# Mamba block with gated experts on one core: the second block's first stages earlier in the written-out order, and the last output stored by chunk

## The chip, the core and the metric

The kernel runs on 1 core of a Trainium2 chip. The core has five engines with a queue of instructions each, worked off in order: TensorE (PE, matrix products and transposes; its weight loads are listed as PEld), VectorE (DVE), ScalarE (ACT, functions from tables that are loaded by an instruction of its own), GpSimd (POOL), and SyncE (SP), which here issues nearly all DMA transfers. Engines wait for one another through semaphores.

The metric is the device time of one execution in microseconds. Before the change it is 2382.32 us, the median of 4 runs (2381.58 to 2382.68).

## What is computed

The input x is 8 sequences of 2048 tokens with 256 channels, all float32. Per sequence, six vectors of modulation (`sa, ca, ga, sb, cb, gb`) come from a condition vector. A Mamba layer (state space model with convolution) and a layer of 8 gated experts follow, each behind a layer norm with modulation, each added to x through a gate:

```python
h = _layernorm(x, axis=-1) * (1 + ca) + sa
x = x + ga * _L0_attn_ref(h, ...)
h = _layernorm(x, axis=-1) * (1 + cb) + sb
x = x + gb * _L0_ffn_ref(h, ...)

# _L0_attn_ref
zxbcdt = hidden_states @ W_in
z, xBC, dt = ...
xBC = jax.nn.silu(_causal_dwconv(xBC, conv_w, conv_b))
dt = jax.nn.softplus(dt + dt_bias)
A = -jnp.exp(A_log)
y = _ssd(x, dt, A, Bm, Cm) + x * D[None, None, :, None]
y = y * jax.nn.silu(z)
y = y * jax.lax.rsqrt(jnp.mean(y * y, axis=-1, keepdims=True) + EPS) * norm_w
return y @ W_out

# _L0_ffn_ref
gate_logits = jax.nn.softmax(x @ gate_w + gate_b, axis=-1)
weights = gate_logits * (gate_logits >= THRESHOLD)
weights = weights / sum(weights)
for e in range(E):
    out = out + weights[:, e:e + 1] * (x @ expert_w[e] + expert_b[e])
```

`_ssd` is the scan over chunks of tokens: within a chunk a masked product of C and B with decays, between chunks a state that is carried on.

## The kernel before

A block is 512 tokens of one sequence (`T`), four chunks of 128 tokens each (`NC`); there are 32 blocks (`order`), four to a sequence. Each block goes through stages, written as generators: `fetch` (the load of x), `first_norm`, `project_xbc` (the six parts of x, B and C, each followed by `conv`, and `steps_of_time` for dt), `project_z`, `silu_xbc`, for each chunk `spread` (the cumulated decays, written to DRAM as `cs_d` and read back to all partitions as `wide`) and `within` (the chunk's products and the state), after each second chunk `outputs`, then `output` (the projection back, added to x), `gate_weights` and `experts`.

No engine chooses what to do. The order is made when the program is built: each stage is put on a list with a due time (`at`), `yield` puts it back by so many units, and `run` always continues the stage that is due first (lines 190 to 204). Blocks start 70 units apart (`PERIOD`, line 802), and each stage has its offset in `STARTS` (line 803). The units are a plan, not microseconds; what they set is the order of the instructions, which the framework may still shift by a few places when it places them on the queues. On the chip an instruction runs when those ahead of it on its engine have been issued and what it waits for is there.

The 8 PSUM banks are handed out by `take` and `give` (lines 211 to 227) in the same plan, with a most for each use (`MOST`).

Lines that the prediction's steps touch:

- Line 107, `load`: a block's x, 512 KB in one transfer. `first_x` comes in four transfers (line 143); `second_x` is loaded on line 160, behind the columns of `w_in` for z (line 149), the head vectors (152) and `d_ch` (156). The queue of SP is shared with all other weights (161 to 175), `cs_d` (505), `wide` (523) and the outputs (761).
- Lines 330, 331, `statistics`, on DVE; 325 and 326, `inv_sqrt`, on POOL; 339, `shift`, on DVE; 343, `xn`, on ACT, four times; 353, transposes on PE; 355, `ht` with the modulation, on ACT, twice. `ht` of the first norm (tag `ht0`) has one buffer, that of the second (`ht1`) two, line 349.
- Line 424: the projection to x, B and C on PE, six times two products of 128x512; 474: dt. Line 379: its first tap with ACT, 383: the last three columns kept as `halo`, 387: three more taps on DVE.
- Line 460: the projection to z, four times two products; 447: its silu on ACT.
- Lines 486 to 515: softplus, cumulated sum (502) and turning of the steps of time, with an exp (490), a log (494) and an exp (507) on ACT.
- Line 442: silu of x, B and C, three times on ACT.
- In `within`: 538 (ACT, one piece of `w` for each of 8 heads), 548, 549, 551 (transposes and C times B on PE), 552 and 553 (exp on ACT), 556 `xdt`, 560 `both`, 572 `w` (DVE), 568 `xdec`, 575 `cw`, 589 `state` (POOL), 586 (PE), 598 and 600 `state` (DVE).
- In `outputs`: 618 (PE), 630 and 634 (DVE), 641 (ACT), 643 and 644 (POOL). In `output`: 659, 672 (PE), 681 (DVE).
- In `gate_weights`: 699, 707, 738 (PE), 734 `wt` (DVE). In `experts`: 778, 791 (PE), 748 (DVE), 756 and 758 (POOL), and the store, line 761, once per block when its last chunk is done.

Functions of different table sets that follow one another on ACT (silu, exp, log) have a load of tables between them, `ACT_TABLE_LOAD`, 1.28 us each in the profile.

Of the kernel before, what the change touches and what calls it, by code (L numbers as in the profile page):

```python
# [15 lines left out]
P = 128  # L16
# [9 lines left out]
def kernel(  # L26
# [26 lines left out]
    nc = tc.nc  # L53
# [6 lines left out]
    KD = DM // P  # L60
# [3 lines left out]
    T = 512  # L64
    NC = T // P
# [7 lines left out]
    def new(pool, shape, tag, bufs=None):  # L73
        n_names[0] += 1
        kw = {} if bufs is None else {"bufs": bufs}
        return pool.tile(shape, F32, tag=tag, name=f"{tag}_{n_names[0]}", **kw)
# [19 lines left out]
    blk = ctx.enter_context(tc.tile_pool(name="block", bufs=2))  # L96
# [4 lines left out]
    order = [(b, s) for b in range(B) for s in range(NSB)]  # L101
# [3 lines left out]
    def load(b, s):  # L105
        xt = new(io, [P, NC, DM], "xt")
        nc.sync.dma_start(out=xt, in_=x[b, ts(s, T), :].rearrange("(c p) d -> p c d", p=P))
        return xt

    def columns(dst, src, first, count):  # L110
        nc.sync.dma_start(
            out=dst, in_=src[:, first : first + count].rearrange("(k p) n -> p k n", p=P)
        )
# [32 lines left out]
    with nc.allow_non_contiguous_dma(reason="small vectors, an element or a few per partition"):  # L146
        nc.sync.dma_start(out=conv_w_sb, in_=conv_w.rearrange("(m p) k -> p m k", p=P))
        nc.sync.dma_start(out=conv_b_sb, in_=conv_b.rearrange("(m p) -> p m", p=P))
        columns(w_in_sb[:, :, :DI], w_in, 0, DI)
        for name, v in (("dt_bias", dt_bias), ("a_log", a_log)):  # L150
            for c in range(NC):
                nc.sync.dma_start(
                    out=heads[name][c * QD : c * QD + NH, :], in_=v.unsqueeze(1)
                )
        for q in range(2):
            nc.sync.dma_start(
                out=d_ch[ts(q, HEADDIM), :],
                in_=d_skip.rearrange("(m q) -> q m", q=2)[q].partition_broadcast(HEADDIM),
            )
        second_x = load(*order[1])  # L160
        nc.sync.dma_start(out=norm_sb, in_=norm_w.rearrange("(m p) -> p m", p=P))
        nc.sync.dma_start(out=wo_n, in_=w_out.rearrange("(m p) o -> p m o", p=P))
        for g, part in enumerate((2, 5)):
            columns(wgate[:, :, g, :], wmod, part * DM, DM)
        columns(wpp[1], wmod, 3 * DM, 2 * DM)
        nc.sync.dma_start(
            out=gate_w_sb[:, :, :NE], in_=gate_w.rearrange("(k p) e -> p k e", p=P)
        )
# [23 lines left out]
    def at(time, stage):  # L192
        heapq.heappush(events, (time, n_events[0], stage))
        n_events[0] += 1
# [16 lines left out]
    def take(use, count=1):  # L211
        while True:
            now = clock[0]
            idle = sorted((t, i) for i, t in enumerate(free_at) if t <= now)
            held = sum(h == use and t > now for h, t in zip(holder, free_at))
            if len(idle) >= count and held + count <= MOST[use]:
                break
            yield 0.2
        got = []
        for _, i in idle[:count]:  # L220
            free_at[i], holder[i] = 1e9, use
            got.append(new(psum, [P, 512], f"bank{i}"))
            bank_of[got[-1].tensor.name] = i
        return got[0] if count == 1 else got

    def give(ps):
        free_at[bank_of.pop(ps.tensor.name)] = clock[0] + READ_TIME
# [26 lines left out]
    def condition():  # L254
        for k in range(KD):
            ps = yield from take("m")
            nc.tensor.transpose(ps[:, :B], cond_sb[:, ts(k, P)], ident[:B, :B])
            nc.scalar.copy(ct[:, k, :], ps[:, :B])
            give(ps)
        yield from modulation(0, 30.0)  # L260

    def warm():


        ps = yield from take("m")
        yield 40.9
        for _ in range(WARM):
            nc.tensor.matmul(ps[:, :P], ones, upper, start=True, stop=True)
        give(ps)

    def modulation(half, later=1.0):
        ps = yield from take("m")
        for n in range(2):
            for d in range(KD):
                for k in range(KD):
                    nc.tensor.matmul(
                        ps[:, ts(n * KD + d, B)], wpp[half][:, k, n * DM + d * P :][:, :P],
                        ct[:, k, :], start=(k == 0), stop=(k == KD - 1),
                    )
        yield later  # L280
        for n in range(2):
            nc.vector.tensor_scalar(
                mod_pp[:, 2 * half + n], ps[:, ts(n, KD * B)].rearrange("p (d b) -> p d b", b=B),
                float(n), None, ALU.add,
            )
        give(ps)
# [35 lines left out]
    def inv_sqrt(res, src, scale):  # L322

        n = res.shape[1]
        nc.gpsimd.tensor_scalar(res, src, scale, EPS, ALU.mult, ALU.add)
        nc.gpsimd.tensor_tensor(res, res, neg_half[:, :n], ALU.pow)
# [6 lines left out]
    def modulated(src, mv, b, half, keep):  # L333

        rstd = new(sml, [P, NC], "rstd")
        inv_sqrt(rstd, mv[:, :, 1], 1.0)
        yield 3.0
        shift = new(sml, [P, NC], "shift")
        nc.vector.scalar_tensor_tensor(shift, mv[:, :, 0], -1.0, rstd, ALU.mult, ALU.mult)  # L339
        yield 1.5  # L340
        xn = new(blk, [P, NC, DM], "xn", bufs=1)
        for c in range(NC):
            nc.scalar.activation(  # L343
                xn[:, c, :], src[:, c, :], AF.Identity,
                bias=shift[:, c : c + 1], scale=rstd[:, c : c + 1],
            )
            yield 0.6
        yield 6.0
        ht = new(blk, [P, KD, T], f"ht{half}", bufs=1 + half)
        for d in range(KD):  # L350
            ps = yield from take("m")
            for c in range(NC):
                nc.tensor.transpose(ps[:, ts(c, P)], xn[:, c, ts(d, P)], ident)  # L353
            yield 1.0
            nc.scalar.activation(  # L355
                ht[:, d, :], ps, AF.Identity,
                bias=mod_pp[:, 2 * half, d, b : b + 1],
                scale=mod_pp[:, 2 * half + 1, d, b : b + 1],
            )
            give(ps)  # L360
            yield 0.8
        yield 1.0
        keep["ht", half] = ht
# [155 lines left out]
    def spread(n, c):  # L519

        yield from until(info[n], "cs_d")
        wide = info[n]["wide", c] = new(chk, [P, NH, P], "wide")
        nc.sync.dma_start(
            out=wide, in_=info[n]["cs_d"][c * QD : c * QD + NH, :].partition_broadcast(P)
        )
        yield
# [162 lines left out]
    def gate_weights(n):  # L689
        b, s = order[n]  # L690
        d = info[n]
        yield from until(d, *(("x1", c) for c in range(NC)))
        yield from modulated(d["x"], d["mv"], b, 1, d)
        ht = d["ht", 1]
        yield 4.0
# [48 lines left out]
    def weighted(n, c, e, ps, res):  # L744
        wt = info[n]["wt"]
        per = 512 // DM
        for q in range(per):
            nc.vector.scalar_tensor_tensor(  # L748
                res, ps[:, ts(q, DM)], wt[:, c, e + q : e + q + 1], res, ALU.mult, ALU.add
            )  # L750
            if q == per - 1:
                give(ps)
            yield 0.5
        if e + per == NE:
            b, s = order[n]
            nc.gpsimd.tensor_mul(res, res, gated[b][1][:, 0, :])  # L756
            x1 = info[n]["x"]
            nc.gpsimd.tensor_add(x1[:, c, :], x1[:, c, :], res)
            if c == NC - 1:
                yield 1.5  # L760
                nc.sync.dma_start(
                    out=out[b, ts(s, T), :].rearrange("(c p) d -> p c d", p=P), in_=x1
                )

    def experts(n):
# [38 lines left out]
        (fetch, -20.0), (first_norm, -9.0), (project_xbc, 11.5), (project_z, 42.0),  # L804
        (silu_xbc, 47.5), (output, 128.0), (gate_weights, 156.0), (experts, 198.0),
    )
    at(-30.0, condition())
    at(-30.0, warm())
    at(12.0, head_weights())
# [3 lines left out]
    for n in range(len(order)):  # L813
        start = n * PERIOD
        for stage, delay in STARTS:
            at(start + delay, stage(n))
        if order[n][1] == 0:
            at(start + 40.0, batch_gates(order[n][0]))
        for c in range(NC):
            at(start + c * PERIOD / NC + 44.0, spread(n, c))  # L820
            at(start + c * PERIOD / NC + 54.0, within(n, c))
# [34 lines left out]
```

## Time and profile before

| what | value |
|---|---|
| median of 4 runs | 2382.32 us |
| the profiled execution | 2381.58 us |
| its span, first to last instruction | 2379.8 us |
| PE busy | 2316.2 us, 97% |
| VectorE, ScalarE, GpSimd busy | 76%, 68%, 47% |
| PE busy in the first 20 us | 13.40 us |
| granted PE clock, mean of the span | 0.993 |
| costliest group, experts' products L791 | 962.4 us in 2048 instructions |
| DMA, mean rate | 46 GB/s |

A line of a timeline has the start in us from the start of the span, the duration, the engine, the line of the kernel, the operation, the tiles and shapes, how many instructions are drawn together, and in brackets how long the engine was idle before and what ended the wait. A matmul in float32 is two instructions. The busy time of an engine is an average over stages with different limits; what a change in one stage is worth is read from that stage. Durations in a merged line overlap a little, since instructions are pipelined.

### The profile page before, as it was taken

To read this page: it belongs to the slowest core of one execution; us is meant where nothing else is said; L and a number is where in the kernel's file an instruction comes from. 1 tells how busy PE (TensorE), PEld (TensorE's weight loads), DVE (VectorE), ACT (ScalarE), POOL (GpSimd) and SP (SyncE) were. 2 spreads that over 40 slices of the span, in tenths; PEclk is the share of its full clock that TensorE was granted. 3 is DMA by queue.
4 is the path that set the end of the run, shared out by engine and by line. 5 is a ranking of instruction groups with operands and counts; after the bars stand their busy time and mean duration, and the time that the engine had idled before them with its cause. 6 is when DMAs were issued, how large, how long until landed. Compare 5 with 4: busy or idle time off the path is not lost.

```text
span 2379.8 us, 33341 instructions
## 1 busy us (share of the span) xinstructions
PE 2316.2 (97%) x11632; PEld 1313.1 (55%) x11632; DVE 1816.9 (76%) x4188; ACT 1621.1 (68%) x2950; POOL 1128.1 (47%) x1245
## 2 busy tenths in 40 slices
PE   7889999999999999999999999999999999999998
PEld 4555555555555555555555555555555555555564
DVE  5777877778777787877787777778777787777775
ACT  6878766677666686666776667766776767667720
POOL 3554445453454454454544554544545444545442
PEclk8999999999999999999999999999999999999999
DMA  5111111110111111111110111111111101111100
GB/s 166 46 37 46 38 46 46 45 55 28 46 55 46 45 46 37 46 54 47 45 46 28 55 55 36 55 37 37 55 45 46 46 29 54 46 45 46 38 19 18
DMA packets 64649, 110.50 MB, mean 46 GB/s; under 512 B 7097, under 2 KB 47073, under 8 KB 64481
## 3 DMA queue, kind: packets, MB, share of 16 engines
q1 hardware_dynamic: 64464, 108.35, 13.8%
q8 instruction: 93, 1.52, 0.3%
q14 instruction: 76, 0.61, 0.1%
q10 hardware_dynamic: 16, 0.01, 0.0%
HBM read 89.47 MB, written 18.87 MB: 46 GB/s over the span
## 4 chain that ended last, share of the span: by engine, by line
PE 61%; ACT 10%; POOL 9%; DVE 6%; issue 1%; POOLq 0%; ACTq 0%; DVEq 0%
PE bank L791 26%; PE bank L672 8%; PE bank L424 7%; PE bank L460 6%; PE bank L618 4%; POOL cw L575 3%; PE bank L586 3%; ACT w L538 3%; DVE xbc L387 2%; PE bank L353 1%; PE bank L548 1%; ACT xbc L442 1%; POOL sq L643 1%; POOL xdec L568 1%; ACT wide L552 1%
## 5 line engine op out<-in xcount | busy, mean ns | idle before, releaser
L791 PE MATMUL bank<-we_sb,ht 128*128 128x512 f32 x2048 | 962.4, 595 | 3.3 <-DVE both L560 1.9
L748 DVE SCALAR_TENSOR_TENSOR res<-bank,wt,res 128x256 f32<-128x256 f32 x1024 | 487.5, 476 | 199.8 <-PE bank L791 113.3
L791 PEld LDWEIGHTS bank<-we_sb,ht 128*128 128x128 f32 x2048 | 373.9, 190 | 379.4 <-issue 352.2
L387 DVE SCALAR_TENSOR_TENSOR xbc<-bank,conv_w_sb,xbc 128x511 f32<-128x511 f32 (+2 forms) x576 | 425.8, 740 | 121.1 <-ACT halo L383 119.6
L575 POOL TENSOR_TENSOR cw<-wide,xbc 128x1024 f32<-128x1024 f32 x128 | 310.8, 2428 | 295.5 <-ACT wide L552 168.9
L538 ACT ACTIVATE w<-wide,tok_major 128x128 f32<-128x128 f32 x1024 | 327.9, 390 | 141.8 <-PE bank L618 100.8
L424 PE MATMUL bank<-ht,w_in_sb 128*128 128x512 f32 x768 | 369.5, 604 | 0.9 <-DVE xbc L387 0.8
L460 PE MATMUL bank<-ht,w_in_sb 128*128 128x512 f32 x512 | 244.4, 601 | 0.0
L672 PE MATMUL bank<-wo,zs 128*128 128x256 f32 x1024 | 243.6, 380 | 0.0
L589 POOL TENSOR_TENSOR state<-state,wide 128x512 f32<-128x512 f32 x112 | 121.7, 1086 | 232.9 <-DVE state L600 206.6
L424 PEld LDWEIGHTS bank<-ht,w_in_sb 128*128 128x128 f32 x768 | 140.7, 192 | 154.9 <-issue 139.8
L355 ACT ACTIVATE ht<-bank,mod_pp 128x512 f32<-128x512 f32 x128 | 97.4, 775 | 178.9 <-PE bank L353 178.7
L379 ACT ACTIVATE xbc<-bank,conv_b_sb,conv_w_sb 128x512 f32<-128x512 f32 x192 | 147.2, 766 | 102.7 <-PE bank L424 102.6
L672 PEld LDWEIGHTS bank<-wo,zs 128*128 128x128 f32 x1024 | 189.8, 191 | 49.0 <-issue 23.5
L568 POOL TENSOR_TENSOR xdec<-xdt,tok_major 128x512 f32<-128x512 f32 x120 | 139.8, 1165 | 141.9 <-DVE xdt L556 141.5
L756 POOL TENSOR_TENSOR res<-res,gates 128x256 f32<-128x256 f32 x128 | 134.8, 1053 | 151.8 <-DVE res L748 144.4
L343 ACT ACTIVATE xn<-xt,shift,rstd 128x256 f32<-128x256 f32 x256 | 137.5, 592 | 82.2 <-DVE shift L339 82.1
L572 DVE TENSOR_TENSOR w<-w,both 128x1024 f32<-128x1024 f32 x128 | 191.9, 1499 | 1.4
L630 DVE SCALAR_TENSOR_TENSOR bank<-xbc,d_ch,bank 128x128 f32<-128x128 f32 x512 | 175.6, 350 | 19.7 <-PE bank L618 10.5
L586 PE MATMUL bank<-xdec,both 128*128 128x512 f32 x240 | 128.7, 618 | 17.6 <-POOL xdec L568 12.7
L460 PEld LDWEIGHTS bank<-ht,w_in_sb 128*128 128x128 f32 x512 | 91.3, 191 | 96.4 <-issue 91.0
L643 POOL TENSOR_TENSOR sq<-sq 128x256 f32<-128x256 f32 x128 | 98.0, 766 | 91.3 <-ACT sq L641 73.4
(130 smaller groups left out, 3331.8 us busy)
## 6 DMA issues: line engine op xcount, KB each, us to landing
wide<-cs_d SPq DMA_DIRECT2D x128, 512.0 KB
out_dram<-xt SPq DMA_DIRECT2D x32, 512.0 KB
xt<-_attn_hidden_states_dram SPq DMA_DIRECT2D x31, 512.0 KB
cs_d<-cs SPq DMA_DIRECT2D x32, 64.0 KB
we_sb<-in_L_ffn_expert_w_dram SPq DMA_DIRECT2D x8, 256.0 KB
ht<-in_L_wmod_dram SPq DMA_DIRECT2D x2, 512.0 KB
w_in_sb<-in_L_attn_W_in_dram SPq DMA_DIRECT2D x1, 776.0 KB
xt<-_attn_hidden_states_dram SPq DMA_DIRECT2D x4, 128.0 KB
```

What stands on the lines that cost most here:

```text
L387: nc.vector.scalar_tensor_tensor(acc[:, ahead:], ps[:, : T - ahead], conv_w_sb[:, m, k : k + 1], acc[:, ahead:], ALU.mult, ALU.add,)
L424: nc.tensor.matmul(ps, w_in_sb[:, k, DI + m * P : DI + (m + 1) * P], ht[:, k, :], start=(k == 0), stop=(k == KD - 1),)
L460: nc.tensor.matmul(ps, w_in_sb[:, k, ts(m, P)], ht[:, k, :], start=(k == 0), stop=(k == KD - 1),)
L538: nc.scalar.activation(w[:, h, :], wide[:, h, :], AF.Relu, bias=tok_major[:, 1, c, h : h + 1], scale=-1.0)
L568: nc.gpsimd.tensor_tensor(by_head(xdec), by_head(xdt), per_head(tok_major[:, 2, c, :]), ALU.mult)
L572: nc.vector.tensor_tensor(w, w, sm[:, None, :].to_broadcast([P, NH, P]), ALU.mult)
L575: nc.gpsimd.tensor_tensor(cw, wide, ct_[:, None, :].to_broadcast([P, NH, P]), ALU.mult)
L586: nc.tensor.matmul(st_ps[:, :DI], bm, xdec, start=True, stop=True)
L630: nc.vector.scalar_tensor_tensor(y[:, m, :], xbc[:, m, tok], d_ch[:, m : m + 1], y[:, m, :], ALU.mult, ALU.add,)
L672: nc.tensor.matmul(o_ps[:, :DM], d["zs"][:, m, ts(c, P)], wo[:, m, :], start=(m == 0), stop=(m == MI - 1),)
L748: nc.vector.scalar_tensor_tensor(res, ps[:, ts(q, DM)], wt[:, c, e + q : e + q + 1], res, ALU.mult, ALU.add)
L791: nc.tensor.matmul(ps, ht[:, k, ts(c, P)], we_sb[:, k, e : e + per, :].rearrange("p e o -> p (e o)"), start=(k == 0), stop=(k == KD - 1),)
```

## The change

Two parts. The second block (`n == 1`) gets its own due times: `first_norm` 57 units earlier, `project_xbc` 38, `project_z` 32, `silu_xbc` 25. So that its x is there, its load is moved on SP ahead of the columns for z, and `ht0` gets a second buffer (the pool's two) for all blocks. And the last block's output is stored chunk by chunk, each as soon as it is added, instead of once. No operation is added or taken away but these stores, three more; the table loads on ACT follow from the order.

```diff
         nc.sync.dma_start(out=conv_b_sb, in_=conv_b.rearrange("(m p) -> p m", p=P))
+        second_x = load(*order[1])
         columns(w_in_sb[:, :, :DI], w_in, 0, DI)
...
-        second_x = load(*order[1])
         nc.sync.dma_start(out=norm_sb, in_=norm_w.rearrange("(m p) -> p m", p=P))
...
-        ht = new(blk, [P, KD, T], f"ht{half}", bufs=1 + half)
+        ht = new(blk, [P, KD, T], f"ht{half}")
...
-            if c == NC - 1:
+            if n == len(order) - 1:
+                nc.sync.dma_start(out=out[b, s * T + c * P :, :][:P], in_=x1[:, c, :])
+            elif c == NC - 1:
                 yield 1.5
...
+
+    AHEAD = {first_norm: 57.0, project_xbc: 38.0, project_z: 32.0, silu_xbc: 25.0}
...
-            at(start + delay, stage(n))
+            at(start + delay - (AHEAD.get(stage, 0.0) if n == 1 else 0.0), stage(n))
```

Built, the changed program has the same instructions as before on PE, DVE and POOL. Their order differs on PE, DVE, ACT and POOL in the work of the first three to four blocks and is the same behind it; on SP in the first loads and the last stores.

## The prediction

> **What bounds the kernel now.** I read the page first, then the table of stretches of 20 us, then the timelines of PE, ACT, DVE and POOL up to 180 us, and the end of the span.
>
> ```profile
> PE 2316.2 (97%) x11632; PEld 1313.1 (55%) x11632; DVE 1816.9 (76%) x4188; ACT 1621.1 (68%) x2950; POOL 1128.1 (47%) x1245
> ```
>
> PE is the bound: 2379.8 - 2316.2 = 63.6 us idle in all. A change that removes no PE work can gain only from that idle time, from half-clock time, or from what follows the last matmul. The stretches say where it lies (after the length: PE, PEld, DVE, ACT, POOL busy, then the granted clock):
>
> ```profile
> 40.00:60.00 20.00, 11.22 (x42) 5.24 (x40) 10.48 (x28) 13.57 (x21) 7.15 (x8) 0.66 0.31 102
> 60.00:80.00 20.00, 16.66 (x85) 8.10 (x85) 16.94 (x30) 18.06 (x40) 11.03 (x7) 0.91 0.13 41
> 120.00:140.00 20.00, 17.59 (x104) 9.48 (x104) 19.27 (x40) 19.91 (x42) 9.70 (x15) 1.00 0.17 57
> 140.00:160.00 20.00, 16.19 (x75) 8.86 (x72) 12.71 (x33) 16.63 (x30) 9.78 (x11) 0.91 0.06 26
> ```
>
> The seven stretches from 20 to 160 us hold 115.95 us of PE work, so 24.05 us idle, most of it in 40 to 60, where a mean clock of 0.66 means 0.34 x 20 / 0.5 = 13.6 us at half speed. But ACT is busy up to 19.9 of 20 afterwards: in this stage it is the second bound. From 160 us on PE is nearly full, so what the change wins must be won before. PE's timeline names the stalls:
>
> ```profile
> 43.84 0.33 PE L549 MATMUL bank<-ident,xbc 128*128 128x128 f32 x1 [2.93 <-ACT xbc L442]
> 48.15 2.05 PE L586 MATMUL bank<-xdec,both 128*128 128x512 f32 x2 [3.42 <-DVE both L560]
> 52.54 0.66 PE L618 MATMUL bank<-w,xdt 128*64 128x128 f32 x2 [2.35 <-DVE w L572]
> 59.21 1.13 PE L424 MATMUL bank<-ht,w_in_sb 128*128 128x512 f32 x2
> ```
>
> PE waits for the first block's silu, mask product and weights, and the second block's projection (L424) starts only at 59.21.
>
> **The norm and the load, moved.** In the changed program's order the second block's statistics stand on DVE before the first `dtv` (DVE was idle 8.21 us there), its four `xn` on ACT after the first L355, where ACT waited 1.39 us until 18.47. Its load goes ahead of the z columns: about 2 us (512 KB at some 250 GB/s) more before these, which L460 reads only at 33. The two rstd steps on POOL fall into 7.93 us of idle time. So 2.06 us of `xn` leave ACT's busy stretch at 48 for nothing. The price: `a_neg` with its table load (1.28 + 0.20) now follows the first L379, ahead of the first exp; DVE's second convolution then ends near 27.1 instead of 26.2, and `cs` and its store 0.8 us later. On SP two more expert loads (0.72 each: 5.04 / 7) stand ahead of `wide`: it starts near 30.4 instead of 28.23 and, with the 5.7 us to its first reader at 33.92, lands near 36.1, just when ACT gets to it (each us later costs one). Net to the third silu: 43.7 against 43.8, nothing won.
>
> **First stall: nothing won either.** The third block's statistics still stand ahead of `both`, and `shift` meets the POOL product:
>
> ```profile
> 44.09 2.35 POOL L575 TENSOR_TENSOR cw<-wide,xbc 128x1024 f32<-128x1024 f32 x1
> 44.15 2.31 DVE L339 SCALAR_TENSOR_TENSOR shift<-mv,rstd 128x4 f32<-128x4 f32 x1 [0.82 <-POOL rstd L326]
> 47.59 0.74 DVE L560 TENSOR_TENSOR both<-bank,masks 128x256 f32<-128x256 f32 x2
> ```
>
> A 128x4 operation took 2.31 us while POOL ran L575. After: the third x lands at 42.9 as now, statistics to 44.7, POOL's two steps to 46.1, then L575 and the blocked shift to 48.4. `both` is 0.8 us later than 47.59, and with it L586 (0 if L575 doesn't meet the shift, then 2.3 us better; each us that the third load is late costs one). Behind `both` in DVE's queue stand state, w and xdt; PE waits for all three.
>
> **Projection and z, moved (38 and 32 us).** They stand on PE right behind the first three L618, before the second chunk's. These start at 53.1; at half speed the first projection ends near 57.0, where ACT's L379 came at 64.42 before: 7.4 us ahead. Its L460, which now stand between 80.93 and 93.4, are interleaved with it and go forward too. Each silu of z now stands between exps and logs on ACT, so the order costs table loads. The row:
>
> ```profile
> 43.80 1.28 ACT L553 ACT_TABLE_LOAD   x1
> 45.09 1.06 ACT L553 ACTIVATE w<-w 128x1024 f32<-128x1024 f32 x1
> 46.17 1.28 ACT L447 ACT_TABLE_LOAD   x1
> ```
>
> From the first L355 to the third block's three silus (L442, ending at 148.2) ACT has 22 loads before and 25 after: 3 x 1.28 = 3.8 us. Up to the second block's silu it is even five more, so that one ends near 97.7 against 96.3.
>
> The Trainium skill speaks against this: "ScalarE: Activation LUTs", section "What ACT_TABLE_LOAD costs", puts each switch at 1.283 us plus 1.38 us of drain, 2.66 us. The rows show the 1.28 and no drain: the activation starts 0.01 us behind the load, the next load 0.02 us behind the activation. By the page the three loads would cost 8.0 us, and the forecast below would be 4.1 us worse.
>
> **The sum of the front, on ACT.** Between 15.57 and 148.2 ACT's idle rows before are 1.39, 1.02, 0.33, 1.89, 1.55, 6.31, 1.76, 3.58, 1.33 and 1.04: 20.2 us. After, walking the changed order with the durations of these timelines, I find 0.9 (to the first L379), 2.1 (second convolution), 6.25 (from 50.75 to the projection at 57.0), 1.9 (third block's first L379, which PE delivers at 110.2) and 0.7 of crumbs: 11.8 us. Ahead of the silu five more `w` pieces (5 x 0.29 = 1.5 us) are done. Gain at the third block's silu: 20.2 - 11.8 - 3.8 - 1.5 = 3.1 us. PE's own count agrees roughly: the third block's second L424, at 117.30 before, comes near 113. Behind it, before, PE lost 2.00 us to `wt` (L738) with its half-clock after; after, L734 and L738 stand ahead of the stalled transposes, so these 2.0 us go (bounds 0 and 3.7, with 3.41 us at half speed saved). Front: 5.1 us. Past that both orders are the same on every engine up to the last store, so nothing pays it back, and PE is full.
>
> **The second ht buffer.** L355's idle time over all blocks is 178.9 us, 178.7 of it ended by the transposes L353, none by the z projection that reads ht: 0, also without cover, since its bound is the remaining 0.2 us.
>
> **The last store.**
>
> ```profile
> 2374.75 0.72 POOL L758 TENSOR_TENSOR xt<-xt,res 128x256 f32<-128x256 f32 x1
> 2375.50 0.37 SPq L761 DMA_DIRECT2D out_dram<-xt  x1
> GB/s 0 0 0 0 0 0 0 0 0 0 0 0 0 0 0 0 0 0 0 0 0 0 0 0 0 82 365 340 348 348 348 262 4 0 0 0 0 0 33 0
> ```
>
> (The last row is 2370 to 2380 in slices of 0.25 us.) 524 KB at 348 GB/s take 1.5 us, from 2376.4 to 2378.0. After, three chunks leave while PE still works (their L758 end near 2355, 2361.8 and 2368.7), and a quarter remains: 0.4 us. Gain 1.1 us (bounds 0, if a store's landing has a floor, and 1.5, all of it). Three more starts at 0.4 us on SP find it empty.
>
> "DMA: Bandwidth & Descriptors", section "Rules for kernel authors", would have small transfers coalesced; the first x here, four loads of 128 KB started in 1.82 us, is there for DVE at 2.90. By that rule the split gains nothing and the sum would be 1.1 us worse; but only the last piece is on the path.
>
> **Sum:** 5.1 + 1.1 = 6.2 us. The profiled execution took 2381.58 (its span 2379.8 and 1.8 around it), 0.74 below the median of the runs. 2381.58 - 6.2 = 2375.4, plus 0.74: 2376.1 us.
>
> **Rivals.** (A) ACT gives it back: the front yields 0 to 1.5 us. For it: between 57 and 108 my ACT has no gap left, and the second block's silu is 1.4 us later. Against: before, ACT loses 3.58 us right behind that silu waiting for POOL's squares, which change place. Time: 2382.3 - 1.1 - 0.5 = 2380.7. (B) Slower: the first block's chunks are pushed back. Second-block work stands ahead of the fourth chunk's exp (82.3 before, 88.6 after by my count, 6.3 us late), and PE's L618 for that chunk stays at 89.9 against 89.54 only because DVE had been later. If nothing done early shortens what follows, 6.3 us are lost less 1.1: 2387.5. It decides if the third block's second L424 starts after 117.3. (C) More: the shift misses L575 (2.3) and the clock is back 3.4 us earlier (1.7): 2376.1 - 4.0 = 2372.1.
>
> **How the numbers follow.** Forecast 0.5, A 0.32, B 0.08, C 0.1. The forecast's own range is 2373.5 to 2378.5. The whole reaches down to C with the other half of `wt`'s bound (2370.4) and up to no front gain with a smaller tail gain (2382.3). A measurement here can't tell less than 0.2% (4.8 us) from none: faster means below 2377.55. That holds for 0.47 of the forecast's 0.5 and C's 0.1: 0.57. Slower is B's upper half with a little from misjudged loads: 0.06. The same: 0.37.
>
> **What would show it.** Right: second block's L424 at 53 to 54, its first L379 at 57; the third block's second L424 near 113; ACT with three more loads before 160; PE idle before 160 shorter by some 5 us and the same after; last bytes 0.4 us behind the last issue's start of data. Wrong: `both` past 50, a third x landing past 45, a clock of 0.5 beyond 58.5, or new idle time on PE after 160.

## The result, and the profile after

The changed kernel takes 2386.09 us, the median of 38 runs (2383.05 to 2390.95), beside 2382.51 before (median of 58, of which two, at 2689 and 9394 us, lie far off and are left out of the ratio). The ratio is 1.0017, with a 95% interval of 1.0013 to 1.0022: about 4 us slower, where 6.2 us faster were forecast, and above the range's upper end of 2382.3. The profiled execution took 2383.86 us, its span 2382.1.

In the changed kernel the numbers of the lines behind the new stores are up by two: its L793 and L780 are L791 and L778 before. The stretches of 20 us of the changed kernel (after the length: PE, PEld, DVE, ACT, POOL busy, granted clock, DMA share, GB/s):

```profile
40.00:60.00 20.00, 12.64 (x50) 6.35 (x49) 10.55 (x21) 13.94 (x22) 5.38 (x5) 0.66 0.30 99
60.00:80.00 20.00, 17.81 (x84) 9.28 (x83) 15.04 (x30) 19.80 (x29) 7.35 (x6) 1.00 0.09 30
80.00:100.00 20.00, 13.15 (x94) 9.57 (x93) 16.43 (x26) 19.25 (x37) 12.60 (x16) 0.83 0.15 54
120.00:140.00 20.00, 16.36 (x64) 7.92 (x62) 16.01 (x30) 18.66 (x40) 12.80 (x11) 0.91 0.13 43
140.00:160.00 20.00, 15.62 (x104) 9.11 (x105) 13.71 (x39) 16.12 (x31) 10.26 (x17) 0.99 0.13 40
```

One stretch of before:

```profile
80.00:100.00 20.00, 17.52 (x112) 10.48 (x110) 17.21 (x30) 18.25 (x29) 11.11 (x13) 1.00 0.13 45
```

PE does more than before up to 80 us. In the stretch from 80 it does less, 13.15 us instead of 17.52, and in those from 120 as well, 16.36 and 15.62 instead of 17.59 and 16.19. The timeline of PE has the stalls (after the line that starts at 53.23, the second block's projection; then the first block's fourth chunk):

```profile
48.67 2.04 PE L586 MATMUL bank<-xdec,both 128*128 128x512 f32 x2 [2.40 <-DVE both L560]
53.23 1.12 PE L618 MATMUL bank<-w,xdt 128*64 128x128 f32 x6 [1.66 <-DVE xdt L556]
54.27 3.37 PE L424 MATMUL bank<-ht,w_in_sb 128*128 128x512 f32 x4
...
93.41 1.97 PE L618 MATMUL bank<-w,xdt 128*64 128x128 f32 x16 [4.92 <-DVE w L572]
95.17 1.92 PE L618 MATMUL bank<-cw,state 128*64 128x128 f32 x16
...
148.31 0.27 PE L738 MATMUL bank<-ident,wt 128*128 128x128 f32 x1
...
153.67 0.38 PE L659 MATMUL bank<-ident,sqs 128*128 128x128 f32 x2
155.67 0.33 PE L659 MATMUL bank<-ident,sqs 128*128 128x128 f32 x1 [1.62 <-POOL sqs L644]
158.28 0.33 PE L659 MATMUL bank<-ident,sqs 128*128 128x128 f32 x1 [2.28 <-POOL sqs L644]
158.44 1.02 PE L793 MATMUL bank<-we_sb,ht 128*128 128x512 f32 x2
159.30 1.70 PE L586 MATMUL bank<-xdec,both 128*128 128x512 f32 x2
160.80 2.94 PE L672 MATMUL bank<-wo,zs 128*128 128x256 f32 x8
```

The same place in the kernel before:

```profile
150.81 0.47 PE L738 MATMUL bank<-ident,wt 128*128 128x128 f32 x1 [2.00 <-DVE wt L734]
151.08 0.64 PE L551 MATMUL bank<-xbc 128*128 128x128 f32 x2
151.50 1.91 PE L791 MATMUL bank<-we_sb,ht 128*128 128x512 f32 x2
...
156.55 0.60 PE L659 MATMUL bank<-ident,sqs 128*128 128x128 f32 x4
156.99 1.02 PE L586 MATMUL bank<-xdec,both 128*128 128x512 f32 x2
157.85 1.89 PE L672 MATMUL bank<-wo,zs 128*128 128x256 f32 x8
```

The wait for `wt` is gone, as forecast. Behind it PE now waits 1.62 and 2.28 us for the second block's squares, which it found ready before, and then runs at half speed: the same eight L672 take 2.94 us instead of 1.89. They end at 163.7 instead of 159.7, and the distance stays: the first block's last chunk is added at 229.1 (225.1 before), the sixteenth's at 1316.9 (1312.9), the last at 2378.62 (2374.75). What POOL does ahead of that wait:

```profile
150.18 2.36 POOL L575 TENSOR_TENSOR cw<-wide,xbc 128x1024 f32<-128x1024 f32 x1 [5.73 <-ACT xbc L442]
152.50 1.70 POOL L643 TENSOR_TENSOR sq<-sq 128x256 f32<-128x256 f32 x1
154.16 1.04 POOL L568 TENSOR_TENSOR xdec<-xdt,tok_major 128x512 f32<-128x512 f32 x1
155.16 0.45 POOL L644 TENSOR_TENSOR sqs<-sq 128x128 f32<-128x128 f32 x1
155.70 0.19 POOL L325 TENSOR_SCALAR rstd<-mv 128x4 f32<-128x4 f32 x1
155.97 1.02 POOL L326 TENSOR_TENSOR rstd<-rstd,neg_half 128x4 f32<-128x4 f32 x1
156.97 0.72 POOL L643 TENSOR_TENSOR sq<-sq 128x256 f32<-128x256 f32 x1
157.76 0.46 POOL L644 TENSOR_TENSOR sqs<-sq 128x128 f32<-128x128 f32 x1
```

The squares of the second block stand in POOL's queue behind the third block's `cw`, which waits for the third block's silu (ends at 150.1). So the last of them ends 8.1 us behind that silu. Before, they stood behind `cw` too and the last ended 7.5 us behind the silu, but PE, held by `wt`, came to them only at 156.55:

```profile
148.36 2.35 POOL L575 TENSOR_TENSOR cw<-wide,xbc 128x1024 f32<-128x1024 f32 x1 [0.58 <-ACT xbc L442]
155.32 0.45 POOL L644 TENSOR_TENSOR sqs<-sq 128x128 f32<-128x128 f32 x1
```

The third block's silu itself, before and in the changed kernel:

```profile
145.33 2.95 ACT L442 ACTIVATE xbc<-xbc 128x1024 f32<-128x1024 f32 x3
147.15 2.95 ACT L442 ACTIVATE xbc<-xbc 128x1024 f32<-128x1024 f32 x3
```

It ends 1.8 us later. From its end to the end of the second block's first L681 are 14.2 us instead of 12.0. These two make up the 4.0.

The end of the program, changed kernel (the last row: 2372 to 2382 in slices of 0.25 us):

```profile
2378.62 0.72 POOL L758 TENSOR_TENSOR xt<-xt,res 128x256 f32<-128x256 f32 x1
2379.37 0.33 SPq L760 DMA_DIRECT2D out_dram<-xt  x1
GB/s 0 0 0 0 0 82 360 115 0 0 0 0 0 0 0 0 0 0 0 0 0 0 0 0 0 0 0 0 0 0 0 0 41 348 135 0 0 0 0 0
```

Three slices of data instead of seven: from the start of the last add to the end of the span 3.5 us instead of 5.0, a gain of 1.5.

### The profile page after: what moved, and what is told of

Its sections match the earlier page's. It is cut to its first block, busy times and chain, and to the rows that moved or that the text cites. A ratio compares the mean times of both kernels' runs of the same rounds, so it can differ in the third digit from the quotient of the medians.

```text
span 2382.1 us, 33349 instructions
## 1 busy us (share of the span) xinstructions
PE 2317.2 (97%) x11632; PEld 1316.5 (55%) x11632; DVE 1816.6 (76%) x4188; ACT 1625.2 (68%) x2953; POOL 1128.0 (47%) x1245
## 4 chain that ended last, share of the span: by engine, by line
PE 61%; ACT 10%; POOL 9%; DVE 6%; issue 1%; POOLq 0%; ACTq 0%; DVEq 0%
PE bank L793 26%; PE bank L672 8%; PE bank L424 7%; PE bank L460 6%; PE bank L618 4%; POOL cw L575 3%; PE bank L586 3%; ACT w L538 3%; DVE xbc L387 2%; PE bank L353 1%; PE bank L548 1%; ACT xbc L442 1%; POOL xdec L568 1%; POOL sq L643 1%; ACT wide L552 1%
## 5 line engine op out<-in xcount | busy, mean ns | idle before, releaser
L793 PE MATMUL bank<-we_sb,ht 128*128 128x512 f32 x2048 | 961.6, 595 | 3.7 <-DVE both L560 2.8
L793 PEld LDWEIGHTS bank<-we_sb,ht 128*128 128x128 f32 x2048 | 373.7, 190 | 380.0 <-issue 352.0
L387 DVE SCALAR_TENSOR_TENSOR xbc<-bank,conv_w_sb,xbc 128x509 f32<-128x509 f32 (+2 forms) x576 | 426.0, 741 | 124.9 <-ACT halo L383 123.2
L575 POOL TENSOR_TENSOR cw<-wide,xbc 128x1024 f32<-128x1024 f32 x128 | 310.6, 2427 | 306.5 <-ACT wide L552 176.0
L424 PE MATMUL bank<-ht,w_in_sb 128*128 128x512 f32 x768 | 369.1, 603 | 0.8 <-DVE xbc L387 0.8
L672 PE MATMUL bank<-wo,zs 128*128 128x256 f32 x1024 | 244.1, 381 | 0.3 <-DVE xt L681 0.3
L424 PEld LDWEIGHTS bank<-ht,w_in_sb 128*128 128x128 f32 x768 | 140.8, 191 | 156.2 <-issue 141.5
L379 ACT ACTIVATE xbc<-bank,conv_b_sb,conv_w_sb 128x512 f32<-128x512 f32 x192 | 147.2, 767 | 107.2 <-PE bank L424 107.2
L672 PEld LDWEIGHTS bank<-wo,zs 128*128 128x128 f32 x1024 | 190.7, 192 | 50.2 <-issue 24.2
L568 POOL TENSOR_TENSOR xdec<-xdt,tok_major 128x512 f32<-128x512 f32 x120 | 141.8, 1182 | 144.4 <-DVE xdt L556 144.1
L572 DVE TENSOR_TENSOR w<-w,both 128x1024 f32<-128x1024 f32 x128 | 190.7, 1490 | 3.3 <-ACT w L553 1.6
L630 DVE SCALAR_TENSOR_TENSOR bank<-xbc,d_ch,bank 128x128 f32<-128x128 f32 x512 | 176.2, 350 | 14.3 <-PE bank L618 5.0
L586 PE MATMUL bank<-xdec,both 128*128 128x512 f32 x240 | 128.2, 616 | 19.2 <-POOL xdec L568 15.4
L618 PE MATMUL bank<-w,xdt 128*64 128x128 f32 x2048 | 138.1, 278 | 6.6 <-DVE w L572 4.9
```

What stands on the lines that cost most here:

```text
L387: nc.vector.scalar_tensor_tensor(acc[:, ahead:], ps[:, : T - ahead], conv_w_sb[:, m, k : k + 1], acc[:, ahead:], ALU.mult, ALU.add,)
L424: nc.tensor.matmul(ps, w_in_sb[:, k, DI + m * P : DI + (m + 1) * P], ht[:, k, :], start=(k == 0), stop=(k == KD - 1),)
L572: nc.vector.tensor_tensor(w, w, sm[:, None, :].to_broadcast([P, NH, P]), ALU.mult)
L575: nc.gpsimd.tensor_tensor(cw, wide, ct_[:, None, :].to_broadcast([P, NH, P]), ALU.mult)
L586: nc.tensor.matmul(st_ps[:, :DI], bm, xdec, start=True, stop=True)
L618: nc.tensor.matmul(y_ps[ts(q, HEADDIM), ts(m, P)], lhs[:, ts(h, HEADDIM)], rhs[:, h, :], start=(i == 0 and m == 0), stop=(i == len(parts) ...
```

## The experiments

Each was timed in five rounds beside the kernel before on the same chip. In the diffs, `AHEAD`, `at` and `after` set due times in the units of the plan. A kernel with other due times has another order of instructions.

**The parts alone.**

`store_alone`, before with the last store split:

```diff
-            if c == NC - 1:
+            if n == len(order) - 1:
+                nc.sync.dma_start(out=out[b, s * T + c * P :, :][:P], in_=x1[:, c, :])
+            elif c == NC - 1:
```

> Before, with the last block's output stored chunk by chunk and nothing else. Theory (only the last piece is on the path): 1.0 to 1.5 us faster than before, about 2381.2 beside 2382.3, nothing changed ahead of 2350 us. Rival (a landing has a floor, small transfers gain nothing): 0 to 0.5 us either way. If the slowdown of the changed kernel came from the stores, this one would be 3 to 5 us slower.

`front_alone`, the changed kernel without that edit:

> The changed kernel with the last output stored once, as before. Theory (all the loss is in the first 170 us): slower than before by the 4.0 us plus what the stores gain, 5 to 6 us (ratio about 1.0022), with the fourth chunk's first L618 on PE at 93.4 behind an idle stretch of 4.9 us. Rival (the loss has to do with the stores at the end): within 1 us of before.

`norm_alone`, as `front_alone`, and

```diff
-    AHEAD = {first_norm: 57.0, project_xbc: 38.0, project_z: 32.0, silu_xbc: 25.0}
+    AHEAD = {first_norm: 57.0}
```

> Only the second block's load and first norm ahead, with the second ht0 buffer; projection, z and silu at their old due times, one store at the end. On ACT the loads of tables between the first block's second w and its fourth are three (before: three, changed: nine). Theory (the nine loads and the z silus ahead of the fourth chunk's exp make the stall): that exp is at 79 to 81, PE does not wait 4.9 us for w, and the time is 0 to 2 us below before (2.06 us of xn leave ACT's busy stretch). Rival (the moved load and norm delay the first block): first stall on PE longer by 2 us or more, 3 to 5 us slower than before.

`no_z`, as `front_alone`, with `AHEAD = {first_norm: 57.0, project_xbc: 38.0, silu_xbc: 25.0}`:

> The changed kernel without the move of the z projection (due as before), one store at the end: load, norm, projection to x, B, C and its silu are ahead. Up to the fourth chunk's w ACT has five loads of tables after the second chunk's start in place of nine and one z silu in place of four: 4 x 1.28 + 3 x 0.6 = 6.9 us less. Theory: the fourth chunk's w on ACT at 82 instead of 88.7, the 4.9 us stall of PE at 88 to 93 gone, and the time 4 to 9 us below the changed kernel's front, 2377 to 2382. Rival (work of the projection itself, its convolutions on ACT and DVE, pushes the chunks back): stall of 3 us or more stays, and the time is 2385 or more.

`xbc10`, as `front_alone`, with `AHEAD = {first_norm: 57.0, project_xbc: 10.0, silu_xbc: 10.0}`:

> Load and norm of the second block ahead, its projection to x, B, C and the silu of it 10 units ahead (instead of 38 and 25), z as before, one store at the end. At 10 units the softplus of the second block (L490, L494) still stands behind both exps of the first block's second chunk, from 15 on it stands between them; ACT has three loads of tables up to the fourth chunk's w, like the kernel with the norm alone. Theory (what counts is how much of the second block's ACT work stands ahead of the first block's last chunks): 2379 to 2382, like the norm alone. Rival (any move of the projection costs, by PE's order or by the clock): 2384 or more.

| kernel | median, us | before beside it | ratio, 95% interval |
|---|---|---|---|
| store_alone | 2380.97 | 2382.44 | 0.9996 (0.9987 to 1.0005) |
| front_alone | 2387.20 | 2382.44 | 1.0024 (1.0014 to 1.0033) |
| norm_alone | 2380.68 | 2382.44 | 0.9993 (0.9984 to 1.0002) |
| no_z | 2387.20 | 2382.44 | 1.0021 (1.0012 to 1.0030) |
| xbc10 | 2382.95 | 2382.81 | 1.0001 (0.9992 to 1.0010) |

The loss is in the front, and in one part of it. With the norm and load alone nothing is lost (neither this gain nor that of `store_alone` is clear of its interval). With the projection to x, B and C and its silu moved too (`no_z`, 38 and 25 units) the time is 6.5 us above that. The move of z, which brings most table loads, adds nothing. My expectation of `no_z` was wrong: the fourth chunk's exp ended at 86.5 instead of 92.0 in `front_alone`, and no time came back. PE waited 3.86 us for that chunk's `xdec` instead. `xbc10` came out between its theory and its rival: 10 units cost about 2 us beside the norm alone (the two intervals overlap), 38 cost 6.5.

**The table loads.** In `after_noload` and `before_noload`, for `n == 1`:

```diff
-        nc.scalar.activation(info[n]["zs"][:, m, :], ps, AF.Silu)
+        nc.scalar.activation(info[n]["zs"][:, m, :], ps, AF.Relu if n == 1 else AF.Silu)
...
-        nc.scalar.activation(ln, u, AF.Ln)
+        nc.scalar.activation(ln, u, AF.Relu if n == 1 else AF.Ln)
```

> The changed kernel, with the silu of the second block's z and the log in its softplus replaced by Relu, a function of every table set (leaves out that silu and that log). Nine loads of tables between the second chunk's start and the fourth chunk's w become one: 8 x 1.28 = 10.2 us of ACT less, in nearly the same order. Theory (the loads make the fourth chunk late): its exp at 80 or before instead of 88.7, no stall of 4.9 us on PE, 2378 to 2382, 4 to 7 us faster than the changed kernel. Rival (it is where the projection and its convolutions stand, with their loads or without): 2384 to 2387.

> The same replacement in the kernel before (leaves out the second block's z silu and the log in its softplus): four loads of tables less, of which two stand ahead of the fourth chunk's w. Theory (here the loads are hidden by ACT's and PE's other waits for the most part): 0 to 3 us faster than before. Rival (ACT's time sets the end of the front one to one): 5 us faster.

Measured: 2386.25 (1.0016, 1.0007 to 1.0025) and 2389.14 (1.0024, 1.0015 to 1.0033). In the changed kernel without the loads the fourth chunk's exp is early:

```profile
79.68 1.05 ACT L552 ACTIVATE wide<-wide 128x1024 f32<-128x1024 f32 x1
80.63 1.05 ACT L553 ACTIVATE w<-w 128x1024 f32<-128x1024 f32 x1
```

It ends at 81.7 instead of 89.8, no L618 waits for `w`, and the time is the same. That the loads cost nothing is not shown by this. Without them the order differs as well: on PE from 68 us on in the changed kernel, from 84 us on in the one before. `before_noload`, with less work, is 6.3 us slower than before, and the only explanation I have is this other order, which wasn't tried apart. In its profile PE waits 1.53 and 1.67 us for the same squares at L659, which come up again below. Such a loss may hide a gain by the loads in `after_noload`.

**The stall at 88 us.** `after_fill` puts PE work into it; `c4_early`, `c34_early` and `dt_late` bring the first block's chunks forward or take the second block's softplus out of their way:

```diff
+            if n == 0 and first + j == 3:
+                for _ in range(4):
+                    nc.tensor.matmul(y_ps, ones, xbc[:, 0, :], start=True, stop=True)
```

> The changed kernel with four products of 128x512 added on PE ahead of the fourth chunk's first L618, written to its bank and overwritten (3.8 to 4.0 us of PE in the stall of 4.92 us). Theory of the clock (the stall's price is its length and then half the time at half speed): no half clock at 91.4 to 98.3, L618 of that chunk 1.1 instead of 1.97 us, 2 to 3.4 us faster than the changed kernel, 2383 to 2384. Rival (half clock there is hidden by ACT or DVE, which set the pace): 2386, within 1 us of the changed kernel.

```diff
-            at(start + c * PERIOD / NC + 54.0, within(n, c))
+            at(start + c * PERIOD / NC + 54.0 - ((0, 0, 0, 10)[c] if n == 0 else 0), within(n, c))
```

> The changed kernel with the first block's fourth chunk due 10 units earlier in the plan and nothing else: on ACT its two exps now stand ahead of the second block's last three L379 instead of behind them, with the same nine loads of tables ahead. Theory (the fourth chunk's late exp stalls PE 4.92 us, and PE, full behind it, brings the third block late by that): exp at 84 to 86 instead of 88.7, the stall 0 to 2 us, the third block's second L424 at 114 to 115.5, and the time 2 to 3.5 us less than the changed kernel's, 2382.5 to 2384. Rival (other chains are as late: the second block's silu, DVE, POOL's xdec): the stall goes and comes back behind it, 2385 to 2387.

The same with `(0, 0, 10, 10)[c]`:

> The changed kernel with the first block's third and fourth chunks both due 10 units earlier: on ACT the exps of both stand ahead of the second block's last five L379, with seven loads of tables ahead of the fourth instead of nine. Theory (the first block's last chunks come first): fourth exp at 80 to 82, no stall at L618, 2380.5 to 2383, 3 to 5.5 us less than the changed kernel. Rival (other chains are as late): 2385 to 2387, and the second block's silu, pushed back by what was moved ahead of it, is at 101 or later.

```diff
-                after(1.9, steps_of_time(n))
+                after(9.9 if n == 1 else 1.9, steps_of_time(n))
```

> The changed kernel with the second block's steps of time (softplus) 8 units later in the plan: its exp and log no longer stand between the two exps of the first block's second chunk, six loads of tables up to the fourth chunk's exp instead of nine. Theory of the place (what stands ahead of the first block's chunks counts): second chunk's w 3.5 to 4 us earlier (exp done at 62 to 63 instead of 66.4), fourth exp 3 to 4 us earlier, 2382 to 2384. Rival: no gain, 2385 to 2387, because PE waits for the second block's dt instead (L511).

| kernel | median, us | ratio, 95% interval | L618 of the fourth chunk waits |
|---|---|---|---|
| changed | 2386.09 | 1.0017 (1.0013 to 1.0022) | 4.92 |
| after_fill | 2384.92 | 1.0012 (1.0004 to 1.0021) | 1.44 (beside the filler) |
| c4_early | 2391.50 | 1.0038 (1.0026 to 1.0051) | 2.53 |
| c34_early | 2385.39 | 1.0012 (1.0003 to 1.0020) | 1.01 |
| dt_late | 2384.87 | 1.0009 (1.0000 to 1.0018) | 2.34 |

None of the times came out as its theory had it. `c34_early` is in its rival's range, `after_fill` and `dt_late` lie between theory and rival, and `c4_early` (five runs) is slower than both. In `c34_early` the stall moves on:

```profile
88.97 1.09 PE L618 MATMUL bank<-w,xdt 128*64 128x128 f32 x16 [1.01 <-DVE w L572]
92.34 0.41 PE L659 MATMUL bank<-ident,sqs 128*128 128x128 f32 x2 [1.41 <-ACT wide L552]
...
97.80 1.19 PE L672 MATMUL bank<-wo,zs 128*128 128x256 f32 x2 [2.83 <-DVE zs L634]
105.81 1.13 PE L586 MATMUL bank<-xdec,both 128*128 128x512 f32 x2 [3.06 <-POOL xdec L568]
```

The time does not follow PE's greatest new wait: 1.01 us of it instead of 4.92, and 0.7 us gained, which is inside the intervals. In `c4_early` the second block's silu ends at 106.5 instead of 99.5.

**The squares behind the third block's silu.** The moved kernels share one more thing: `no_z`, `front_alone` and the changed kernel each wait 3.9 us in two pieces at L659 between 140 and 170 us, `norm_alone` 2.3, the kernel before nothing. `after_sqv`, `norm_store_sqv` and `before_sqv` have this edit, the first in the changed kernel:

```diff
-            nc.gpsimd.tensor_add(sq[:, 0:2, :], sq[:, 0:2, :], sq[:, 2:4, :])
-            nc.gpsimd.tensor_add(d["sqs"][:, c, :], sq[:, 0, :], sq[:, 1, :])
+            eng = nc.vector if (n, c) in ((1, 2), (1, 3)) else nc.gpsimd
+            eng.tensor_add(sq[:, 0:2, :], sq[:, 0:2, :], sq[:, 2:4, :])
+            eng.tensor_add(d["sqs"][:, c, :], sq[:, 0, :], sq[:, 1, :])
```

> The changed kernel with the adds of squares (L643, L644) of the second block's last two chunks on DVE instead of POOL; the order on PE and ACT stays. In the changed kernel these four adds stand on POOL behind the third block's cw (L575, 2.36 us), which waits for the third block's silu, and the last ends 8.1 us behind that silu; PE waits 1.62 + 2.28 us for them at L659 and then runs at half speed for 3.41 us. Theory (behind 140 us it is this chain, silu, cw, squares, L659, that PE waits for): the last sqs at 154.5 to 156 instead of 158.2, L659 waits under 1 us, no half clock at 159.7, 3 to 4 us faster than the changed kernel, 2382 to 2383. Rival (PE is held there by something else, the third block's x or its second block's output): within 1 us of it, 2385 to 2387.

> The kernel before with the same four adds of squares (second block, last two chunks) on DVE; the order on PE stays. There PE does not wait at L659 for these (it waits 2.00 us for wt at L738, and comes to L659 at 156.55, the last sqs ending 155.78). Theory (the chain of squares is late only where PE comes to it early): 0 to 1 us faster than before. Rival (the squares on DVE gain with any order): 2 to 4.6 us faster.

`after_fill2` leaves the waits and fills them:

```diff
+            for _ in range((0, 0, 6, 9)[c] if n == 1 else 0):
+                nc.tensor.matmul(s_ps[:, ts(c, P)], ones, upper, start=True, stop=True)
             nc.tensor.transpose(s_ps[:, ts(c, P)], d["sqs"][:, c, :], ident)
```

> The changed kernel with fifteen products of 128x128 added on PE, six ahead of the third and nine ahead of the fourth transpose L659 of the second block, written to places that the transposes overwrite: 1.3 and 2.0 us of PE inside the waits of 1.62 and 2.28 us. Theory of the clock (here nothing but PE sets the pace behind the wait, so half speed counts in full): the 3.41 us at half speed at 159.7 gone, 1.0 to 1.7 us faster than the changed kernel, about 2384.6. Rival (as with the filler in the stall at 88 us, the half speed is hidden or only moves): 2385.5 or more, or slower.

| kernel | median, us | ratio, 95% interval |
|---|---|---|
| after_sqv | 2381.50 | 0.9999 (0.9991 to 1.0008) |
| before_sqv | 2383.00 | 1.0000 (0.9991 to 1.0009) |
| after_fill2 | 2383.91 | 1.0007 (0.9998 to 1.0016) |

Four small adds on another engine take 4.6 us off the changed kernel, and nothing off the kernel before. On PE and ACT `after_sqv` has the same order as the changed kernel. The profile of `before_sqv` says why nothing is gained there (the edit adds a line, so L739 and L660 are L738 and L659):

```profile
152.27 0.33 PE L739 MATMUL bank<-ident,wt 128*128 128x128 f32 x1 [2.00 <-DVE wt L735]
158.10 0.60 PE L660 MATMUL bank<-ident,sqs 128*128 128x128 f32 x4
```

PE waits for `wt` first and finds the squares ready, wherever they are added. `after_sqv` in its profiled execution, one of its slower runs at 2384.2:

```profile
155.69 0.59 PE L660 MATMUL bank<-ident,sqs 128*128 128x128 f32 x3
158.69 0.47 PE L660 MATMUL bank<-ident,sqs 128*128 128x128 f32 x1 [2.41 <-DVE sqs L645]
```

One wait of 2.41 is left of two, since the adds wait on DVE as well, and half speed still follows it in this run. From the end of the third silu to the end of the first L681 of the second block are 12.4 us, 14.2 in the changed kernel: 1.8 us that the profiles show. The rest of the 4.6 is not shown. Eight of the eleven runs of `after_sqv` took 2379.7 to 2381.9 us, and the profiled one is of the other three. If no half speed follows the wait in those eight, that is worth 1.7 us more (an estimate, 3.41 / 2). `after_fill2` points that way: the waits were filled, no half speed came behind them, and the median fell by 2.2 us though PE had more to do. But its interval overlaps that of the changed kernel.

**A version that beats both.** `norm_store` is `norm_alone` with the split store; `norm_store_sqv` adds the squares on DVE.

> Only the parts of the change that gained alone: the load and the norm of the second block ahead (with the second ht0 buffer) and the last output by chunk; projection, z and silu due as before. Theory (the two gains add, since one lies ahead of 160 us and the other behind 2350): 1.76 + 1.47 = 3.2 us less than before, 2379.2. Rival (the norm's gain was the clock's phase in those runs): only the stores' 1.0 to 1.5 us.

> The kernel with the load and norm ahead and the last output by chunk, with the same four adds of squares on DVE. There PE waits 0.65 + 1.67 us at L659. Theory of the chain: most of that goes, 1 to 2.3 us less than 2379.3, 2377 to 2378.3, 4.4 to 5.7 us less than before. Rival (no gain where PE has other work in front): 2379 to 2380.

Measured: 2379.30 (0.9985, 0.9976 to 0.9994) and 2377.32 (0.9978, 0.9968 to 0.9987), the latter 5.2 us below the kernel before. In the latter's profile one short wait is left, and no half speed between 130 and 550 us:

```profile
152.40 0.49 PE L660 MATMUL bank<-ident,sqs 128*128 128x128 f32 x3
153.50 0.33 PE L660 MATMUL bank<-ident,sqs 128*128 128x128 f32 x1 [0.60 <-DVE sqs L645]
154.53 1.89 PE L673 MATMUL bank<-wo,zs 128*128 128x256 f32 x8
```

## Why the prediction was wrong

Two terms of the sum failed. ACT's sum was to bring the third block's silu 3.1 us forward, and it came 1.8 us later. The wait at L738 was to give 2.0 us, and behind the silu 2.2 us were lost. In detail:

- **Norm and load, "nothing won" to the third silu.** That silu ended at 44.7 instead of 43.8, with a wait of 2.10 us ahead of the first L379 where 0.9 was counted. Alone, with the projection left where it was, the move gave 1.8 us (not beyond its interval): with the norm ready, the projection starts at 57.29 without being due earlier.
- **First stall, 0.8 us later.** Right in kind, 0.5 us: `both` starts at 48.11 instead of 47.59 behind a `shift` that took 2.30 us beside L575, and L586 comes at 48.67.
- **Projection at 53 to 54, first L379 at 57.** Nearly right: 54.27 and 57.69.
- **Three more table loads, and 1.5 us of `w` pieces ahead.** Counted right: 25 loads against 22, and ACT's work up to the third block's silus is 116.9 us instead of 111.7, 5.2 more where 5.3 were forecast. Whether this price belongs in the sum stays open: without the loads the time was the same, in another order.
- **"11.8 us" of idle time on ACT, hence a gain of 3.1.** This step failed. ACT's rows of waits add up to 16.9 us: 1.2 more at the start, and 5.7 instead of 1.9 at the third block, for which PE came late. With what was measured the sum is 20.2 - 16.9 - 5.2 = -1.9, and the third silu ended at 150.1, not 145.1. The walk gave ACT's rows the times of PE and DVE before, as if these delivered whenever ACT was ready. The two longest of the third block's waits:

```profile
105.99 0.78 ACT L355 ACTIVATE ht<-bank,mod_pp 128x512 f32<-128x512 f32 x1 [1.54 <-PE bank L353]
114.29 0.78 ACT L379 ACTIVATE xbc<-bank,conv_b_sb,conv_w_sb 128x512 f32<-128x512 f32 x1 [2.37 <-PE bank L424]
```

- **L618 of the fourth chunk "stays at 89.9".** Failed: the exp came at 88.7 as forecast, but `w` then stood on DVE behind L630 and L634 and was done at 93.4. That was rival B's mechanism, and its point of decision (third block's second L424 after 117.3) came with 117.52; its 2387.5 is 1.4 us from the measured time. Still, with the stall shortened to 1.0 us the time fell by 0.7, so that B's time comes close is in part luck.

```profile
88.72 1.04 ACT L553 ACTIVATE w<-w 128x1024 f32<-128x1024 f32 x1
90.78 0.69 DVE L634 TENSOR_TENSOR zs<-bank,zs 128x512 f32<-128x512 f32 x1
91.39 1.97 DVE L572 TENSOR_TENSOR w<-w,both 128x1024 f32<-128x1024 f32 x1
```

- **L738: "so these 2.0 us go".** They went, and a wait in the second block's output stage took their place: 3.9 us at L659 and 1.7 us of half speed (3.41 / 2). The bound of this term, 0 to 3.7 us of gain, should have reached below nothing: what PE meets next behind `wt` was to be looked up, and the squares, last ready at 155.78 before, were only 0.8 us ahead of PE. `after_sqv` and `before_sqv` put this at 4.6 us of the 5.1 that the changed front loses against `store_alone`. Rival A's paragraph did name POOL's squares, at 102 us instead of here.
- **The same order behind, nothing paid back.** Right: from 164 us on the distance stays at 3.9 to 4.0 us.
- **The second ht buffer, 0.** Not run alone.
- **The store, 1.1 us.** 1.5 alone by the medians (not clear of its interval), 1.5 by the profiles: the bound, all of it. No loss by the smaller transfers shows.

What stays open: with the squares on DVE in both, the moves of projection, z and silu still cost 4.2 us (2381.50 against 2377.32). No single edit found that part. It seems to go with the third block's silu, which ends 0.5 to 8.6 us later than before in the profiles with the projection moved, and within 0.8 us of it in those with the norm alone. But that is argued from profiles, not tried, and the profile of `front_alone` has this silu 3.6 us later than that of the changed kernel, with the same order up to there.

## What to carry to other kernels

A gain in the middle of several engines' queues is not read from one engine's idle time. For each wait that goes, look up what the same engine waits for next and how long that was ready before: here 0.8 us, and behind it a queue that the change couldn't shorten. Where a plan sets the order, try each moved stage by itself before adding them up; of the parts of this change only two, the norm with its load and the split store, were worth having (together 0.9985, clear of its interval).

## What the runs showed of the hardware

- **Half speed without a long gap.** At L659 neither wait reaches 2.3 us, but with 0.33 us of work between them they were followed by 3.41 us at half speed, from 159.5 on; in `after_sqv` a single wait of 2.41 us was, from 158.4 on; with the waits filled (`after_fill2`) no half speed followed. In every trace here the stretches at half speed, but for the one cut off by the end, last one to five times 3.41 us, as the Trainium skill has it ("TensorE: Matmul & The Clock Gate", section "What's actually happening": a free-running window of 3413 ns). Its advice to leave no idle gap above some 3 us (section "Why this matters for your kernels") would have called these two waits harmless.
- **What filling brings.** Filling the waits at 155 us brought 2.2 us (`after_fill2`), filling the stall at 88 us 1.2 (`after_fill`). Neither is clear of the changed kernel's interval, so a difference between the two places is not shown.
- **Scatter that goes with the clock.** The changed kernel's runs follow the granted clock: six at a mean of 0.995 took 2383.7 us on average, ten at 0.991 took 2389.4, with the same instructions. The kernel before shows none of it (2382.4 at 0.993, 2383.1 at 0.995). What sets the clock of a run is not shown.
- **VectorE beside POOL.** The same `w` of 128x1024 on VectorE (L572) took 1.22 us at 51.36 and 66.46, where POOL did nothing, and 2.56 us at 79.12, begun while L575 was running. At 137.90 it took 1.22 us, and POOL's `xdec` (L568), begun 0.08 us behind it, 2.04 instead of 1.04.
